# The Newton step of two layer norms moves from GpSimd to VectorE, in four fused operations

## The chip, the cores and the metric

The kernel runs on one core of one Trainium2 chip. The metric is the device time of one execution in microseconds (us); of several executions the median is taken. Engines are named as in the profile: PE is TensorE (matrix products), DVE is VectorE, ACT is ScalarE, POOL is GpSimd and SP is SyncE, which issues most of the transfers. PEld is TensorE's loading of weights, which runs beside its products.

## What is computed

The input x has 4 images of 64 x 64 tokens with 256 channels. Two layers follow each other. Cut to what matters:

```python
# layer 0: attention over the 4096 tokens of an image
f, g, v = xt @ Wf, xt @ Wg, xt @ Wh               # 32, 32 and 128 channels
beta = softmax(g @ f.T)                           # 4096 x 4096
x = x + (beta @ v) @ Wo

# layer 1: triangle attention, 8 heads of 32 channels, on the 64 x 64 grid of tokens
q, k, v1, v2 = x @ Wq, x @ Wk, x @ Wv1, x @ Wv2
att = softmax(einsum('bilhd,bljhd->biljh', q, k) / sqrt(32), axis=2)
out = einsum('biljh,bilhd,bljhd->bijhd', att, v1, v2)
h = layer_norm(x + out @ Wo)                      # the first norm
h = relu(h @ W1 + b1) @ W2 + b2 + h
return layer_norm(h)                              # the second norm
```

A layer norm needs for each token the mean m and the variance v over its 256 channels, and then r = 1/sqrt(v + eps). The kernel takes a first r from a logarithm and an exponential on ScalarE and improves it with one Newton step, r (1.5 - 0.5 (v + eps) r r). The normed value is r x + (-m r), one ScalarE operation with r and -m r as scale and bias.

## The kernel before

The kernel goes through the images. For each it does the attention, then the triangle, and into the triangle of an image it weaves other work: into that of image 0 the preparation of later images (order ORDER0), and into those of images 1 to 3 the rest of layer 1, the "pieces" of 256 tokens of the image before (order ORDER). The pieces of the last image come at the end, in a closing stage (`alone`).

The triangle of an image has 32 steps. A step makes eight products of a weight tile with v2, each 128 x 2048, and TensorE sums each with four selecting matmuls into PSUM. `npool` gives the last three products of an even step and the last two of an odd step to GpSimd, the others to VectorE. [...] ScalarE copies its share of the weights to SBUF (`copy_weights`).

```python
def product(self, step, m):
    ...
    if m >= 8 - k:                                          # k = npool(step)
        R = work.tile([P, D, N], F32, tag="Rp", name="Rp")  # two buffers
        eng, src = nc.gpsimd, attP[:, m - 8 + k, :]         # weights in SBUF
    else:
        R = work.tile([P, D, N], F32, tag="R", name="R", bufs=3)
        eng, src = nc.vector, att[:, n, ts(h, 64)]          # weights in PSUM
    v2 = self.v2[step // NIG]
    eng.tensor_tensor(R, src.unsqueeze(1).to_broadcast([P, D, N]), v2[:, h], ALU.mult)

def accumulate(self, step, m):
    ...
    for c in range(4):
        nc.tensor.matmul(acc[32 * c : 32 * c + 32, n % 2, :], w[:, n, c, 16 * h : 16 * h + 32], ...)

def copy_weights(self, step):
    ...
    nc.scalar.copy(attP[:, 0:k, :], att.rearrange(...)[:, 8 - k : 8, :])
```

The statistics, the root and the Newton step:

```python
def stats(self, src, k, ns=range(2)):                       # on VectorE
    for n in ns:
        nc.vector.bn_stats(st, src[:, n, :])
        nc.vector.bn_aggr(self.mv[:, k + n, :], st)

def sums_of(self, src, junk, mv, k):                        # on ScalarE: mean / 16, and the variance
    for n in range(2):
        nc.scalar.activation(junk[:, n, :], src[:, n, :], AF.Identity, scale=1.0 / (16 * C),
                             accum_out=mv[:, k + n, 0:1])
    for n in range(2):
        nc.scalar.activation(junk[:, n, :], src[:, n, :], AF.Square, bias=mv[:, k + n, 0:1],
                             scale=-1.0 / 16, accum_out=mv[:, k + n, 1:2])

def polish(self, k0, k1, eng, scale=1.0, back=None):        # the Newton step
    ...
    eng.tensor_scalar(t0, mv[:, :, 1], LN_EPS / scale, -0.5 * scale, ALU.add, ALU.mult)
    eng.tensor_tensor(t1, rs, rs, ALU.mult)
    eng.tensor_tensor(t1, t0, t1, ALU.mult)
    eng.tensor_scalar(t1, t1, 1.5, None, ALU.add)
    ...
    eng.tensor_tensor(r, t1, rs, ALU.mult)
    eng.tensor_tensor(nb, mv[:, :, 0], r, ALU.mult)
    if back is None:
        eng.tensor_scalar(nb, nb, -1.0, None, ALU.mult)
    else:
        eng.tensor_tensor(nb, nb, back[:, k0:k1], ALU.mult)
```

In the triangles of images 1 to 3 the first norm's statistics are taken by `stats`, the second's by `sums_of`, and `polish` runs on GpSimd for both norms at once (four columns). In the closing stage `polish` runs on VectorE with two columns, while GpSimd does `residue` and `finish`, two operations each on 128 x 512 elements.

The order in which the instructions of all engines are recorded is written by hand-made words. In ORDER, `R04/2` is the product m = 4 of the even step of a period, `R16` the product m = 6 of the odd step, `/2` says that it belongs to the work that began two periods earlier. A period is two steps and one piece. The other words: `A..` the summing of a product on TensorE, `T..` the taking of a sum from PSUM, `sp` a quarter of the scores and `e0 e1` their exponentials, `S.` the sums of the softmax, `W.` the weights, `t.` their transposes, `c.` copy_weights, `V.` the copy of v1; of the piece `h0 h1` the heads, `sa so` the statistics of the first and second norm, `rr` the roots, `pp` polish, `fa fo` the two affine operations, `ht` the transposes of the normed tile and `hU hT` what is read out of them, `m. r.` and `z.` the two layers of the perceptron, `fi` finish.

```python
ORDER = """
    r0/1 A10/2 A11/2 m1/1 R14/2 R05/1 S1/1 R15/2 T10/2 sp/1 A14/2 A16/2 r1/1 e0/1 e1/1 A15/2 A05/1 T11/2
    R04/1 A04/1 z0/1 W1/1 R03/1 V1/1 fi/2 S0 z1/1 t1/1 so/1 R06/1 R00/1 c1/1 sa A03/1 R07/1 R02/1 A06/1
    A02/1 A00/1 rr/1 pp/1 W0 R01/1 A07/1 A01/1 fo/1 fa T01/1 R12/1 t0 T00/1 R17/1 h1/-1 R13/1 h0/-1 ht
    R16/1 hU A13/1 hT A12/1 A17/1 R11/1 c0 R10/1 m0 V0
"""
```

Of the kernel before, what the change touches and what calls it, by code (L numbers as in the profile page):

```python
# [10 lines left out]
F32 = mybir.dt.float32  # L11
# [5 lines left out]
P = 128  # L17
# [21 lines left out]


ORDER = """
    r0/1 A10/2 A11/2 m1/1 R14/2 R05/1 S1/1 R15/2 T10/2 sp/1 A14/2 A16/2 r1/1 e0/1 e1/1 A15/2 A05/1 T11/2
    R04/1 A04/1 z0/1 W1/1 R03/1 V1/1 fi/2 S0 z1/1 t1/1 so/1 R06/1 R00/1 c1/1 sa A03/1 R07/1 R02/1 A06/1
    A02/1 A00/1 rr/1 pp/1 W0 R01/1 A07/1 A01/1 fo/1 fa T01/1 R12/1 t0 T00/1 R17/1 h1/-1 R13/1 h0/-1 ht
    R16/1 hU A13/1 hT A12/1 A17/1 R11/1 c0 R10/1 m0 V0
""".split()


# [13 lines left out]
def attention_then_triangle_kernel(  # L62
# [40 lines left out]
    nc.gpsimd.memset(ones_b, 1.0)  # L103
    ones_f = ctile([P, P], "ones_f")
    nc.gpsimd.memset(ones_f, 1.0)
    back_t = ctile([P, 4], "back")
    nc.gpsimd.memset(back_t, -1.0)
    nc.gpsimd.memset(back_t[:, 2:4], -16.0)
    eps_t = ctile([P, 1], "eps")
    nc.gpsimd.memset(eps_t, LN_EPS)  # L110

# [282 lines left out]
    def layer0(b, F, safe, rest):  # L394
# [250 lines left out]
        if old:  # L645
            rest.stats_a(t0)
            rest.roots(0, 2)
            rest.polish(0, 2, nc.gpsimd)
        bounds(last)
        proj(last, "v2", 0, None, stage[1][:, 0, :], nc.scalar)  # L650
        L.fetch_v2(0, 1)
# [234 lines left out]
    class Tokens:  # L886
# [69 lines left out]
                )  # L956


        def roots(self, k0, k1, scale=1.0):
            ln = small.tile([P, 4], F32, tag="ln", name="ln")  # L960
            nc.scalar.activation(ln[:, k0:k1], self.mv[:, k0:k1, 1], AF.Ln, bias=eps_t, scale=scale)
            self.rs = small.tile([P, 4], F32, tag="rs", name="rs")
            nc.scalar.activation(self.rs[:, k0:k1], ln[:, k0:k1], AF.Exp, scale=-0.5)


        def polish(self, k0, k1, eng, scale=1.0, back=None):
            mv, rs = self.mv[:, k0:k1], self.rs[:, k0:k1]
            t = small.tile([P, 2, 4], F32, tag="nt", name="nt")
            t0, t1 = t[:, 0, k0:k1], t[:, 1, k0:k1]
            eng.tensor_scalar(t0, mv[:, :, 1], LN_EPS / scale, -0.5 * scale, ALU.add, ALU.mult)  # L970
            eng.tensor_tensor(t1, rs, rs, ALU.mult)
            eng.tensor_tensor(t1, t0, t1, ALU.mult)
            eng.tensor_scalar(t1, t1, 1.5, None, ALU.add)
            self.rn = small.tile([P, 2, 4], F32, tag="rn", name="rn")
            r, nb = self.rn[:, 0, k0:k1], self.rn[:, 1, k0:k1]
            eng.tensor_tensor(r, t1, rs, ALU.mult)
            eng.tensor_tensor(nb, mv[:, :, 0], r, ALU.mult)
            if back is None:
                eng.tensor_scalar(nb, nb, -1.0, None, ALU.mult)
            else:  # L980
                eng.tensor_tensor(nb, nb, back[:, k0:k1], ALU.mult)
            self.mv = None

        def affine(self, dst, src, k, ns=range(2)):
# [97 lines left out]
        def alone(self, t0, t1):  # L1082
            V = nc.vector

            def normed(k0, k1):
                self.roots(k0, k1)
                self.polish(k0, k1, V)
# [36 lines left out]
            self.outputs(tt, 1, pc)  # L1124

            def summed(n):
                V.tensor_tensor(z[:, n], self.zp[tt + n][:, n], z[:, n], ALU.add)
                self.stats(z, 2, (n,))
                self.roots(2 + n, 3 + n)
                return self.mv, self.rs  # L1130

            def closed(n, known):
                self.mv, self.rs = known
                self.polish(2 + n, 3 + n, V)
# [16 lines left out]
    def step_words(L, fetched, stored):  # L1151
# [37 lines left out]
                L.copy_weights(step)  # L1189

        def scores(j):
            if j == 1:
                scores(0)
                L.take_scores()
            if 0 <= j < 12:
                L.scores(1 + j // 4, j % 4)
                sps[j] = L.sp
                if j % 4 == 3 and j // 4 + 2 < NPAIR:  # L1200
                    L.fetch_qk(j // 4 + 2)

        def take_scores(j, half):
            if 1 <= j < 12:
                L.sp = sps[j]
                L.take_scores(half)

# [8 lines left out]
    def first_layer1(L, ahead, F):  # L1216
# [30 lines left out]
        for period in range(NSTEP // 4 + 3):  # L1247
            for word, late in words_of(ORDER0):
                i, last = period - late, int(word[-1])
                if word[0:2] == "sp":  # L1250
                    if i >= 0:
                        scores(2 * i + 1 + last)
                elif word[0] == "e":
                    if i >= 0:
# [8 lines left out]
    def next_layer1(b, L, rest, ahead, F):  # L1263
# [32 lines left out]
        def of_piece(word, q):  # L1296
# [138 lines left out]
```

## Time and profile before

| | before |
|---|---|
| time, median of 3 runs | 3813.18 us (3807.73 to 3815.09) |
| span of the profiled execution | 3814.4 us |
| PE busy | 3687.0 us |
| DVE busy | 2639.6 us |
| ACT busy | 1930.3 us |
| POOL busy | 1804.2 us |
| accumulations of the triangles of images 0, 1, 2, 3, from and to | 502 to 925, 1379 to 1827, 2283 to 2733, 3187 to 3641 us |

A row of the groups reads: line, engine, operation, output and inputs with their sizes, count | busy time, mean of one in ns | idle time of the engine before them and what ended most of it. A row of a timeline reads: start, duration, engine, line, operation, count, and in brackets the idle time before it. L849 is the products, L859 the summing, L970 to L981 the Newton step, L1076 and L1077 `finish`, L1033 and L1034 `residue`.

### The profile page before, as it was taken

The numbers are of one execution on the slowest core, as the hardware profiler recorded it, in microseconds if no ns is written. First come the engines' busy times: TensorE is split into PE (matmuls) and PEld (weight loads), VectorE is DVE, ScalarE is ACT, GpSimd is POOL, SyncE is SP. The second block draws the span as 40 slices with busy tenths as digits, with TensorE's granted clock in tenths as the row PEclk, the third lists the DMA queues.
The fourth block names the chain that finished last, engine by engine and source line by source line (L and its number), as shares of the span: only waits on it lengthen the run. The fifth ranks groups of instructions, "written<-read, shape, count | busy, mean of one in ns | idle before, by whom it ended". The sixth has DMA issues, their size and how long they took to land.

```text
span 3814.4 us, 60208 instructions
## 1 busy us (share of the span) xinstructions
PE 3687.0 (97%) x23498; PEld 1800.0 (47%) x23498; DVE 2639.6 (69%) x2050; ACT 1930.3 (51%) x4257; POOL 1804.2 (47%) x930
## 2 busy tenths in 40 slices
PE   9999989898999999999999999999999999999997
PEld 5444444443444455554344444555344445555476
DVE  4444479997544459999544448999754455999976
ACT  3333355554333356776333346766533335677654
POOL 4000079996000049999100008999600004999944
PEclk9999999999999999999999999999999999999999
DMA  4111355544111164313111153342211116431221
GB/s 117 54 50 50 95 145 147 142 124 139 38 46 53 53 152 94 89 49 93 61 50 47 53 126 83 83 95 70 92 42 47 50 59 144 95 88 48 69 61 51
DMA packets 439750, 309.44 MB, mean 81 GB/s; under 512 B 299360, under 2 KB 404576, under 8 KB 432160
## 3 DMA queue, kind: packets, MB, share of 16 engines
q1 hardware_dynamic: 419952, 291.12, 29.1%
q10 hardware_dynamic: 16240, 8.59, 0.8%
q0 software_dynamic: 3264, 5.78, 0.7%
q8 instruction: 188, 3.08, 0.4%
q14 instruction: 106, 0.87, 0.1%
HBM read 165.88 MB, written 139.46 MB: 80 GB/s over the span
## 4 chain that ended last, share of the span: by engine, by line
PE 79%; POOL 5%; DVE 5%; DMA 4%; issue 4%; ACT 2%; SPq 1%; ACTq 0%; DVEq 0%; POOLq 0%
PE o L469 24%; PE acc L859 16%; PE proj L526 8%; PE s L447 7%; PE mp L1042 5%; PE zp L1062 4%; POOL Rp L849 4%; DVE R L849 3%; PE v1p L551 3%; PE sp L747 3%; PE hp L918 2%; DMA xin<-in_x_dram 2%; PE y L511 2%; PE att L801 1%; PE den L486 1%
## 5 line engine op out<-in xcount | busy, mean ns | idle before, releaser
L849 POOL TENSOR_TENSOR Rp<-attP,v 128x2048 f32<-128x2048 f32 x328 | 1490.1, 4575 | 459.0 <-ACT attP L809 385.2
L849 DVE TENSOR_TENSOR R<-att,v 128x2048 f32<-128x2048 f32 x696 | 1546.4, 2274 | 111.3 <-PE acc L859 77.8
L476 DVE TENSOR_TENSOR esum<-esum,e 128x2048 f32<-128x2048 f32 x224 | 512.8, 2289 | 586.2 <-ACT e L458 582.6
L859 PE MATMUL acc<-R,wsel 128*32 128x512 f32 x5568 | 706.4, 605 | 37.2 <-DVE R L849 25.5
L458 ACT ACTIVATE e<-s 128x1024 f32<-128x1024 f32 x512 | 496.5, 1021 | 406.5 <-PE s L447 391.9
L970 POOL TENSOR_SCALAR nt<-mv 128x4 f32<-128x4 f32 (+1 forms) x51 | 9.9, 193 | 1286.2 <-DVE mv L935 1282.4
L469 PE MATMUL o<-e,vlo 128*128 128x512 f32 x1024 | 477.0, 609 | 0.0
L469 PE MATMUL o<-e,vhi 128*128 128x512 f32 x1024 | 472.6, 605 | 0.0
L859 PE MATMUL acc<-Rp,wsel 128*32 128x512 f32 x2624 | 349.8, 605 | 12.9 <-POOL Rp L849 12.3
L869 ACT COPY ao<-acc 128x1024 f32<-128x1024 f32 x256 | 254.1, 1020 | 198.0 <-PE acc L859 135.9
L859 PEld LDWEIGHTS acc<-R,wsel 128*32 128x32 f32 x5568 | 153.7, 110 | 370.6 <-issue 269.8
L469 PEld LDWEIGHTS o<-e,vlo 128*128 128x128 f32 x1024 | 185.1, 191 | 283.0 <-issue 283.0
L469 PEld LDWEIGHTS o<-e,vhi 128*128 128x128 f32 x1024 | 184.3, 189 | 279.7 <-issue 279.7
L447 PE MATMUL s<-gT,fT 32*128 32x512 f32 x2048 | 302.2, 640 | 4.3 <-ACT e L458 3.9
L784 ACT ACTIVATE es<-S,rd 128x64 f32<-128x64 f32 x1024 | 257.7, 336 | 3.4 <-ACT stage L538 2.6
L488 DVE RECIPROCAL rec<-den 128x512 f32<-128x512 f32 x32 | 107.4, 3358 | 215.6 <-PE den L486 215.6
L1062 PE MATMUL zp<-w,hid 128*128 128x256 f32 x1024 | 247.6, 387 | 7.5 <-ACT hid L1051 7.5
L1042 PE MATMUL mp<-hT,w 128*128 128x256 f32 x1024 | 249.5, 389 | 0.7 <-ACT hT L1014 0.7
L1042 PEld LDWEIGHTS mp<-hT,w 128*128 128x128 f32 x1024 | 186.5, 190 | 101.9 <-ACT attP L809 36.0
L1062 PEld LDWEIGHTS zp<-w,hid 128*128 128x128 f32 x1024 | 186.5, 191 | 72.2 <-issue 31.9
L538 ACT COPY st<-proj 128x512 f32<-128x512 f32 x104 | 60.9, 585 | 293.2 <-issue 165.9
L859 PEld LDWEIGHTS acc<-Rp,wsel 128*32 128x32 f32 x2624 | 81.3, 111 | 202.0 <-issue 138.2
(166 smaller groups left out, 3832.7 us busy)
## 6 DMA issues: line engine op xcount, KB each, us to landing
v<-v2d SPq DMA_DIRECT2D x24, 1024.0 KB, 12.7
v1c<-v1d SPq DMA_DIRECT2D x128, 128.0 KB, 2.9
aT<-ao SPq DMA_DIRECT2D x1024, 16.0 KB, 1.9
A<-aT SPq DMA_DIRECT2D x256, 64.0 KB, 2.1
out_dram<-z SPq DMA_DIRECT2D x63, 256.0 KB, 2.5
y<-yT SPq DMA_DIRECT2D x56, 256.0 KB, 2.1
q<-st SPq DMA_DIRECT2D x56, 256.0 KB, 2.6
v1d<-st SPq DMA_DIRECT2D x56, 256.0 KB, 2.2
```

The source lines that it names most:

```text
L447: nc.tensor.matmul(s_ps[r // 2][:, r % 2, :], fT[rows, tt, ts(n, P)], gT[rows, ts(qb, QB)], start=True, stop=not safe,)
L458: nc.scalar.activation(e[g][:, 2 * j : 2 * j + 2, :], s_ps[j], AF.Exp)
L469: nc.tensor.matmul(o_ps[qb], F.v[tt][:, r * 4 + n, :], es[:, r, :], start=(k == 0 and r == 0), stop=(k == 7 and r == 3),)
L476: nc.vector.tensor_tensor(esum[qb], esum[qb], es, ALU.add)
L526: nc.tensor.matmul(ps, w[:, cc, rows], y(qb, cc), start=(cc == 0), stop=(cc == 1))
L551: nc.tensor.matmul(ps[:, ts(n, C)], y(qb, cc)[:, ts(m * 2 + n, P)], wv1_sb[:, cc, :], start=(cc == 0), stop=(cc == 1),)
L784: nc.scalar.mul(e[:, i, :], rows[:, i, :], rec[:, i : i + 1])
L849: eng.tensor_tensor(R, src.unsqueeze(1).to_broadcast([P, D, N]), v2[:, h], ALU.mult)
L859: nc.tensor.matmul(acc[32 * c : 32 * c + 32, n % 2, :], w[:, n, c, 16 * h : 16 * h + 32], R[:, ts(c, 8), :].rearrange("p d j -> p (d j)"), ...
L869: nc.scalar.copy(self.ao[step][:, ts(np, 2)].rearrange("p k d j -> p k (d j)"), self.acc[step][np])
L1042: nc.tensor.matmul(self.mp[:, fc % 2, :], w1_sb[:, cc, ts(fc, P)], self.hT[tt][:, cc, :], start=(cc == 0), stop=(cc == 1),)
L1062: nc.tensor.matmul(zp[:, n, :], self.hid[tt][:, fc, ts(n, P)], w2_sb[:, fc, :], start=(fc == 0), stop=(fc == 3 and tt not in self.hT2),)
```

## The change

The Newton step is written as four operations of the form (a op scalar) op b, always on VectorE. The factor that brings the mean back from mean / 16 becomes part of the last of them. For this both norms must have their statistics in the same form, so in the triangles of images 1 to 3 the first norm's are now taken by ScalarE too. This takes the step off GpSimd and the batch-norm statistics off VectorE, and makes the step shorter in operations. The quarters of the scores are numbered from zero, so that each period has one and the first is no exception. The words of ORDER stand in a new order for these new loads. ORDER0, the attention and the image-0 triangle keep theirs.

```diff
 ORDER = """
-    r0/1 A10/2 A11/2 m1/1 R14/2 R05/1 S1/1 R15/2 T10/2 sp/1 A14/2 A16/2 r1/1 e0/1 e1/1 A15/2 A05/1 T11/2
-    ...
+    A12/3 V0/2 sp/2 T10/3 m1/2 e0/2 R17/3 R02/2 e1/2 A02/2 r1/2 R15/3 A16/3 R14/3 A15/3 R00/2 c0/2 A17/3
+    sa/1 A14/3 S0/1 fi/3 R03/2 T11/3 z1/2 S1/1 z0/2 t1/2 R05/2 A03/2 W0/1 R01/2 so/2 rr/2 R04/2 c1/2
+    R06/2 A05/2 pp/2 A01/2 V1/2 A06/2 A00/2 A04/2 R13/2 R10/2 R07/2 fo/2 t0/1 fa/1 R16/2 h1 ht/1 T00/2
+    hU/1 R11/2 h0 A07/2 hT/1 A13/2 R12/2 A10/2 W1/1 T01/2 m0/1 A11/2 r0/1
 """.split()
...
-        def polish(self, k0, k1, eng, scale=1.0, back=None):
-            mv, rs = self.mv[:, k0:k1], self.rs[:, k0:k1]
+        def polish(self, k0, k1, part=1.0):
+            mv, rs, V = self.mv[:, k0:k1], self.rs[:, k0:k1], nc.vector
             ...
-            eng.tensor_scalar(t0, mv[:, :, 1], LN_EPS / scale, -0.5 * scale, ALU.add, ALU.mult)
-            eng.tensor_tensor(t1, rs, rs, ALU.mult)
-            eng.tensor_tensor(t1, t0, t1, ALU.mult)
-            eng.tensor_scalar(t1, t1, 1.5, None, ALU.add)
             ...
-            eng.tensor_tensor(r, t1, rs, ALU.mult)
-            eng.tensor_tensor(nb, mv[:, :, 0], r, ALU.mult)
-            if back is None:
-                eng.tensor_scalar(nb, nb, -1.0, None, ALU.mult)
-            else:
-                eng.tensor_tensor(nb, nb, back[:, k0:k1], ALU.mult)
+            V.scalar_tensor_tensor(t0, mv[:, :, 1], LN_EPS, rs, ALU.add, ALU.mult)
+            V.scalar_tensor_tensor(t1, t0, -0.5, rs, ALU.mult, ALU.mult)
+            V.scalar_tensor_tensor(r, t1, 1.5, rs, ALU.add, ALU.mult)
+            V.scalar_tensor_tensor(nb, mv[:, :, 0], -1.0 / part, r, ALU.mult, ALU.mult)
...
             elif word == "sa" and first:
                 moments(q - 1)
-                rest.stats(rest.hps[t0 + q], 0)
+                h = rest.h[tt] = work.tile([P, 2, C], F32, tag="h", name="h", bufs=1)
+                rest.sums_of(rest.hps[tt], h, rest.mv, 0)
...
             elif word == "pp" and second:
                 moments(q)
                 rest.rs = rs.pop(q)
-                rest.polish(0 if q + 1 < n1 else 2, 4, nc.gpsimd, back=back_t)
+                rest.polish(0 if q + 1 < n1 else 2, 4, 1.0 / 16)
...
                 elif word == "sp":
-                    if i >= 1:
-                        scores(i)
+                    scores(i)
```

More of the change, by code (lines that the diff above doesn't have):

```diff
@@ L41 @@
 ORDER = """
-    r0/1 A10/2 A11/2 m1/1 R14/2 R05/1 S1/1 R15/2 T10/2 sp/1 A14/2 A16/2 r1/1 e0/1 e1/1 A15/2 A05/1 T11/2
-    R04/1 A04/1 z0/1 W1/1 R03/1 V1/1 fi/2 S0 z1/1 t1/1 so/1 R06/1 R00/1 c1/1 sa A03/1 R07/1 R02/1 A06/1
-    A02/1 A00/1 rr/1 pp/1 W0 R01/1 A07/1 A01/1 fo/1 fa T01/1 R12/1 t0 T00/1 R17/1 h1/-1 R13/1 h0/-1 ht
-    R16/1 hU A13/1 hT A12/1 A17/1 R11/1 c0 R10/1 m0 V0
+    A12/3 V0/2 sp/2 T10/3 m1/2 e0/2 R17/3 R02/2 e1/2 A02/2 r1/2 R15/3 A16/3 R14/3 A15/3 R00/2 c0/2 A17/3
+    sa/1 A14/3 S0/1 fi/3 R03/2 T11/3 z1/2 S1/1 z0/2 t1/2 R05/2 A03/2 W0/1 R01/2 so/2 rr/2 R04/2 c1/2
+    R06/2 A05/2 pp/2 A01/2 V1/2 A06/2 A00/2 A04/2 R13/2 R10/2 R07/2 fo/2 t0/1 fa/1 R16/2 h1 ht/1 T00/2
+    hU/1 R11/2 h0 A07/2 hT/1 A13/2 R12/2 A10/2 W1/1 T01/2 m0/1 A11/2 r0/1
 """.split()
@@ L105, in attention_then_triangle_kernel @@
     nc.gpsimd.memset(ones_f, 1.0)
-    back_t = ctile([P, 4], "back")
-    nc.gpsimd.memset(back_t, -1.0)
-    nc.gpsimd.memset(back_t[:, 2:4], -16.0)
     eps_t = ctile([P, 1], "eps")
@@ L647, in layer0 @@
             rest.roots(0, 2)
-            rest.polish(0, 2, nc.gpsimd)
+            rest.polish(0, 2)
         bounds(last)
@@ L956, in sums_of, with roots @@
                 )
[L959 removed]
+        def roots(self, k0, k1):
             ln = small.tile([P, 4], F32, tag="ln", name="ln")
[L961 removed]
+            nc.scalar.activation(ln[:, k0:k1], self.mv[:, k0:k1, 1], AF.Ln, bias=eps_t)
             self.rs = small.tile([P, 4], F32, tag="rs", name="rs")
             nc.scalar.activation(self.rs[:, k0:k1], ln[:, k0:k1], AF.Exp, scale=-0.5)
[L966 to L967 removed]
+        def polish(self, k0, k1, part=1.0):
+            mv, rs, V = self.mv[:, k0:k1], self.rs[:, k0:k1], nc.vector
             t = small.tile([P, 2, 4], F32, tag="nt", name="nt")
             t0, t1 = t[:, 0, k0:k1], t[:, 1, k0:k1]
[L970 to L973, printed above, removed]
             self.rn = small.tile([P, 2, 4], F32, tag="rn", name="rn")
             r, nb = self.rn[:, 0, k0:k1], self.rn[:, 1, k0:k1]
[L976 to L981 removed]
+            V.scalar_tensor_tensor(t0, mv[:, :, 1], LN_EPS, rs, ALU.add, ALU.mult)
+            V.scalar_tensor_tensor(t1, t0, -0.5, rs, ALU.mult, ALU.mult)
+            V.scalar_tensor_tensor(r, t1, 1.5, rs, ALU.add, ALU.mult)
+            V.scalar_tensor_tensor(nb, mv[:, :, 0], -1.0 / part, r, ALU.mult, ALU.mult)
             self.mv = None
@@ L1086, in normed @@
                 self.roots(k0, k1)
-                self.polish(k0, k1, V)
+                self.polish(k0, k1)
             def turn(tt):
@@ L1133, in closed @@
                 self.mv, self.rs = known
-                self.polish(2 + n, 3 + n, V)
+                self.polish(2 + n, 3 + n)
                 self.affine(z, z, 2, (n,))
@@ L1193, in scores @@
         def scores(j):
-            if j == 1:
-                scores(0)
-                L.take_scores()
             if 0 <= j < 12:
@@ L1203, in take_scores @@
         def take_scores(j, half):
-            if 1 <= j < 12:
+            if 0 <= j < 12:
                 L.sp = sps[j]
@@ L1251, in first_layer1 @@
                     if i >= 0:
+                        if i == last == 0:
+                            scores(0)
+                            for half in range(2):
+                                take_scores(0, half)
                         scores(2 * i + 1 + last)
```

## Prediction

> **What bounds the kernel now.** I read the busy table first, then the busy time by stretch, the groups, and the timeline of single engines.
>
> ```profile
> PE 3687.0 (97%) x23498; PEld 1800.0 (47%) x23498; DVE 2639.6 (69%) x2050; ACT 1930.3 (51%) x4257; POOL 1804.2 (47%) x930
> ...
> L849 POOL TENSOR_TENSOR Rp<-attP,v 128x2048 f32<-128x2048 f32 x328 | 1490.1, 4575 | 459.0 <-ACT attP L809 385.2
> L849 DVE TENSOR_TENSOR R<-att,v 128x2048 f32<-128x2048 f32 x696 | 1546.4, 2274 | 111.3 <-PE acc L859 77.8
> ...
> L970 POOL TENSOR_SCALAR nt<-mv 128x4 f32<-128x4 f32 (+1 forms) x51 | 9.9, 193 | 1286.2 <-DVE mv L935 1282.4
> ```
>
> TensorE is busy for 97% of the span, so only its idle 3814.4 - 3687.0 = 127 us can be won. But the averages hide a stage in which three engines are full. The change touches the triangles of images 1 to 3 and the closing stage; a row of the next table is a 50 us stretch with PE, PEld, DVE, ACT and POOL busy.
>
> ```profile
> 1550.00:1600.00 50.00, 50.00 (x472) 27.66 (x468) 48.20 (x36) 35.94 (x98) 47.71 (x28) 1.00 0.41 92
> ...
> 3650.00:3700.00 50.00, 48.90 (x244) 42.46 (x244) 39.49 (x115) 26.37 (x70) 23.40 (x19) 1.00 0.27 73
> ```
>
> In a triangle, VectorE (48.20) and GpSimd (47.71) are within 5% of TensorE (50.00). A period (two steps, one piece of the tokens) takes 27.76 us, the distance between successive Newton steps in GpSimd's timeline; the last four take 27.2. GpSimd's side of one period:
>
> ```profile
> 1511.64 0.20 POOL L981 TENSOR_TENSOR rn<-rn,back 128x4 f32<-128x4 f32 x1
> 1511.79 13.66 POOL L849 TENSOR_TENSOR Rp<-attP,v 128x2048 f32<-128x2048 f32 x3
> 1525.37 1.31 POOL L1076 TENSOR_TENSOR z<-z,log_bc 128x512 f32<-128x512 f32 x1
> 1526.76 1.29 POOL L1077 TENSOR_TENSOR z<-z,lob_bc 128x512 f32<-128x512 f32 x1
> 1528.50 9.10 POOL L849 TENSOR_TENSOR Rp<-attP,v 128x2048 f32<-128x2048 f32 x2 [0.46 <-PE acc L859]
> ```
>
> To be seen: products follow each other without a gap, one per 13.66/3 = 4.55 us. Now what VectorE's small operations cost while GpSimd works, from the closing stage (start, duration, engine):
>
> ```profile
> 3666.71 0.16 DVE L971 TENSOR_TENSOR nt<-rs 128x2 f32<-128x2 f32 x1
> 3666.78 1.27 POOL L1077 TENSOR_TENSOR z<-z,lob_bc 128x512 f32<-128x512 f32 x1
> 3666.91 1.15 DVE L972 TENSOR_TENSOR nt<-nt 128x2 f32<-128x2 f32 x1
> ...
> 3668.01 1.27 POOL L1033 TENSOR_TENSOR z<-h,lag_bc 128x512 f32<-128x512 f32 x1
> ...
> 3668.10 1.20 DVE L973 TENSOR_SCALAR nt<-nt 128x2 f32<-128x2 f32 x1
> 3669.33 0.16 DVE L976 TENSOR_TENSOR rn<-nt,rs 128x2 f32<-128x2 f32 x1
> 3669.35 1.28 POOL L1034 TENSOR_TENSOR z<-z,lb_bc 128x512 f32<-128x512 f32 x1
> 3669.53 1.12 DVE L977 TENSOR_TENSOR rn<-mv,rn 128x2 f32<-128x2 f32 x1
> ```
>
> L972 has two columns and needs 0.16 us when left alone, yet takes 1.15: it ends at 3668.06, when GpSimd's L1077 does (3668.05). L973 and L977 likewise end with L1033 and L1034. GpSimd is not delayed. An operation slips in between (L971, L976) only where GpSimd has a gap, as between L1076 and L1077, the second of which needs the first. Between L1077 and L1033, which start back to back, one VectorE operation gets through and the next waits for the whole of L1033.
>
> **What the Trainium skill says.** "SBUF — State Buffer", section "Who interferes with whom": a VectorE instruction with two SBUF inputs contends with a GpSimd instruction that reads SBUF, and whichever starts second is blocked until the first ends. The trace agrees (1.15 us for a 0.16 us operation). It also explains why VectorE's products (2274 ns) don't suffer: one of their inputs lies in PSUM. "Perfetto Trace Analysis", section "GPSIMD Engine Instruction", advises start-to-start spacing over reported spans; hence 4.55 us here. "VectorE: DVE Perf Modes", section "Rules for kernel authors", says to minimize the number of operations; the change does, but in the triangle it is the wait that counts. "PSUM — Partial Sum Buffer", section "PSUM bank collisions raise a hardware error", forbids ScalarE and VectorE in one bank at once, and the built program keeps to it: a ScalarE copy of weights waits for the VectorE products recorded before it.
>
> **The change part by part.**
> GpSimd loses seven Newton operations a period: 1509.94 to 1511.79 in its timeline, 1.85 us. With them gone its period is 5 x 4.55 + 2.65 = 25.4 us.
> VectorE loses two pairs of statistics, 1532.79 to 1533.95, 1.16 us. It gains four small operations, 0.2 us each in the closing stage (L972 to L973: 3663.15 to 3663.35), 0.8 us if nothing blocks them. ScalarE gains about 1.9 us (the same four statistics of the second norm: 1507.39 to 1509.27) on 19.9 of 27.8; it has room.
> TensorE's work per period is the same, and so is the number of its changes between 32-column and 128-column work (four runs of accumulation in both orders). No gain there. The quarters of the scores move by one word, with all else one period later; I give it nothing.
> So on paper everything but the Newton step gets lighter. But all its four operations read two SBUF tensors (mv and rs, nt and rs, mv and rn), and in the new order they stand behind the product R04 on VectorE while GpSimd does R06, R07 and R16.
>
> The new period, as an estimate from the durations above, with 0 at the end of a Newton step:
> - VectorE does R13, R10, R11, R12, R02, R15, R14, R00: 8 x 2.21 = 17.7 (13.28/6 = 2.21 in its timeline). ScalarE's c0 copies R05's weights out of the same PSUM bank, and in the built program waits for R00: 18.1.
> - R05 starts at 18.2. R05, R06, R07, R16 end at 22.8, 27.3, 31.9 and 36.4, if TensorE frees their buffers in time. It does: from 0 come the norm's affine operations on ScalarE 2.0, ht 0.5, h0 1.1, A07 A13 A10 2.7 (an A is 0.86), m0 1.9, A11 A12 1.9, sp 1.9, m1 1.9, A02 A16 1.9, so A16, which frees R05's buffer, by about 16; A17 by 18, A05 by 25, A06 by 28.
> - VectorE meanwhile: sums 0.8, R03 20.8, sums 0.8, R01 23.8, R04 (needs A03, about 24.1) 26.4. The root is there by 25.4: TensorE's z words end at 22.5, and W0, the statistics and two activations keep ScalarE until then. The first operation arrives in the middle of R06.
> - First operation done at 27.3 with R06, second at 31.9 with R07, third at 36.4 with R16. The next product, R17, needs the buffer of A07, which stands on TensorE behind the transpose of the normed tile, so behind this very step: GpSimd is idle and the fourth passes. End: 36.7 us.
> TensorE then waits some 9 us a period. Its own 27.8 us lie beside this.
> The first and last Newton steps of a triangle stand at 1391.6 and 1813.2 (2297.5 and 2720.9; 3199.7 and 3624.0): 15 distances, 421.6 + 423.4 + 424.3 = 1269.3 us. After: 3 x 15 x 36.7 = 1651.5. Difference +382. Start and end of a triangle: about +5 each for the first blocked step and the later last products, +15.
> Closing stage: seven operations from 3665.51 to 3670.85 become four, of which perhaps three are blocked: 1 to 2 us less per piece. But the piece (10.33 us) holds about 9.9 us of TensorE work, so at most 0.4 x 15 = 6, I take -5.
> Sum: 3813 + 382 + 15 - 5 = 4205.
>
> **Rivals.**
> A: two operations slip through at one boundary. Then the step ends with R07 at about 32.1, 15 x 32.1 = 481.5 per image, +212, near 4020. For it: L971 and L976. Against: these slip where GpSimd has a gap, and products have none.
> B: no blocking of the fused form. Then the chain A02, R00, c0, R05, R06, A06, around TensorE back to A02, is 2.3 + 0.5 + 9.1 + 17.1 = 29.0 us (17.1 being TensorE's 27.8 less the 10.7 from A16 to A01) in the 12 periods with scores, 27.2 without: at most +45, 3810 to 3860. For it: the only fused operation of this kind before (L512, 743 ns) reads PSUM, so the trace has no case. Against: L972 and L977 are blocked for their two SBUF inputs, and the fused ones have them too.
> C: the change works as meant: 1.85 us off GpSimd frees the last four periods and the fill, 3 x 4 x about 1.3 = 16 us, 3795. For it: the last four periods are exactly GpSimd's sum (27.2). Against: as B, and c0.
>
> **Range and chances.** I give about 0.7 to the full blocking (4150 to 4250), 0.2 to A or a mixture, 0.1 to B and C. I put the prediction at 4190, a little under the sum for A's sake; 3990 to 4240 should hold it 8 times in 10. Faster by over 2% 0.01, within 2% 0.07, slower by over 2% 0.92.
>
> **What will show it.** In the changed profile the four fused operations should have means of microseconds instead of 0.2, several near 4.5, and end together with GpSimd's products; the step should come every 36 to 37 us in triangles 1 to 3; TensorE's busy share should fall to about 88%, with waits of ScalarE's norms for rn and of TensorE for h at the transposes. The image-0 triangle and the attention stages should stay as they are. Fused operations of 0.2 us in the triangle would prove me wrong (B); steps every 32 us would be A; and if GpSimd's products rather than VectorE's operations were delayed, the mechanism would be turned around.

## The result and the profile after

The changed kernel takes 4304.56 us (median of 4 runs, 4302.66 to 4310.92) against 3814.14 us (3807.73 to 3815.23) for the kernel before: a ratio of 1.129, 95% interval 1.127 to 1.131. It is slower, as predicted; the size is 114 us above the predicted 4190 and outside the range.

The page of the kernel after, busy times and groups (L846 are the products, L969 to L972 the fused step, L977 the affine operations, L915 the heads' products on TensorE); behind them two rows of the groups with different shapes kept apart:

```profile
PE 3802.0 (88%) x23498; PEld 1862.0 (43%) x23498; DVE 3055.9 (71%) x1974; ACT 2001.9 (47%) x4625; POOL 1728.5 (40%) x571
...
L846 POOL TENSOR_TENSOR Rp<-attP,v 128x2048 f32<-128x2048 f32 x328 | 1483.9, 4556 | 2364.0 <-ACT attP L806 1637.9
L846 DVE TENSOR_TENSOR R<-att,v 128x2048 f32<-128x2048 f32 x696 | 1553.2, 2278 | 176.5 <-PE acc L856 143.2
...
L977 ACT ACTIVATE z<-zp,rn 128x256 f32<-128x256 f32 x98 | 50.0, 560 | 499.9 <-DVE rn L972 499.9
```

```profile
L970 DVE SCALAR_TENSOR_TENSOR nt<-nt,rs 128x4 f32<-128x4 f32 x46 | 203.9, 4433 | 1.6
L971 DVE SCALAR_TENSOR_TENSOR rn<-nt,rs 128x4 f32<-128x4 f32 x46 | 189.4, 4117 | 1.6
```

The second and the third operation have means of 4433 and 4117 ns on four columns, the first and the fourth 1060 and 162 ns. ScalarE's affine operation waits 499.9 us for the step's last result. GpSimd, from the first to the last accumulation of images 1 to 3, is busy for 1178.3 of 1826.7 us, where it was busy for 1262.5 of 1343.5; the 2364 us of idle time in the table include the attention stages. The products themselves cost what they did (4556 and 2278 ns). TensorE's busy time has grown by 115 us for the same 23498 matmuls; the experiments come back to that.

Busy time by stretch (PE, PEld, DVE, ACT, POOL), the same place in a triangle and one in the closing stage:

```profile
1550.00:1600.00 50.00, 34.99 (x283) 19.46 (x272) 47.57 (x24) 24.00 (x67) 32.56 (x9) 0.86 0.12 30
...
4150.00:4200.00 50.00, 50.00 (x252) 43.89 (x251) 34.39 (x93) 27.71 (x74) 25.20 (x20) 1.00 0.30 82
```

VectorE still shows 47.57 of 50 us busy, but much of it is waiting inside its own operations; TensorE has fallen to 34.99 and GpSimd to 32.56. In the timeline of VectorE one sees a whole period's step:

```profile
1660.70 2.29 DVE L846 TENSOR_TENSOR R<-att,v 128x2048 f32<-128x2048 f32 x1 [0.33 <-PE acc L856]
1662.91 0.72 DVE L969 SCALAR_TENSOR_TENSOR nt<-mv,rs 128x4 f32<-128x4 f32 x1
1663.66 4.46 DVE L970 SCALAR_TENSOR_TENSOR nt<-nt,rs 128x4 f32<-128x4 f32 x1
1668.16 4.42 DVE L971 SCALAR_TENSOR_TENSOR rn<-nt,rs 128x4 f32<-128x4 f32 x1
1672.61 0.16 DVE L972 SCALAR_TENSOR_TENSOR rn<-mv,rn 128x4 f32<-128x4 f32 x1
1672.69 6.69 DVE L846 TENSOR_TENSOR R<-att,v 128x2048 f32<-128x2048 f32 x3
1680.77 2.29 DVE L846 TENSOR_TENSOR R<-att,v 128x2048 f32<-128x2048 f32 x1 [1.39 <-PE acc L856]
```

and in that of GpSimd what stands beside it, four products R05, R06, R07, R16 back to back:

```profile
1654.52 18.03 POOL L846 TENSOR_TENSOR Rp<-attP,v 128x2048 f32<-128x2048 f32 x4 [5.83 <-ACT attP L806]
1680.02 4.56 POOL L846 TENSOR_TENSOR Rp<-attP,v 128x2048 f32<-128x2048 f32 x1 [7.46 <-PE acc L856]
```

The four products end near 1659.1, 1663.6, 1668.1 and 1672.55. L969, L970 and L971 end at 1663.63, 1668.12 and 1672.58, so one VectorE operation gets through at each boundary. This holds throughout: all 135 operations on four columns that took over 0.3 us end within 0.03 us of the end of a GpSimd operation. L972 has GpSimd idle and takes 0.16 us. The step takes 9.9 us in place of the 1.85 it took on GpSimd, and everything behind it waits.

From span to span (3814.4 to 4301.8, +487.4 us; a triangle's stretches are taken from TensorE's accumulations and the starts of the steps; the first accumulations of images 1 to 3 before the change are at 1382.4, 2286.6 and 3190.4 us, some 3 us later than the table of the profile before has them):

| stretch | predicted | measured |
|---|---|---|
| 15 distances between steps, images 1 to 3 | +382 | 568.1 + 569.1 + 570.1 - 1269.2 = +438.1 |
| last accumulation of an image to the first of the next, 3 times | together | (464.4 - 457.1) + (465.0 - 458.9) + (463.8 - 456.7) = +20.5 |
| first accumulation to first step, and last step to last accumulation | +15 | +0.8, and 15.6 + 17.2 + 11.7 = +44.5 |
| closing stage, last accumulation to the end | -5 | 173.1 to 159.9 = -13.2 |
| up to the end of image 0's triangle | 0 | 925.2 to 921.9 = -3.3 |

### The profile page after: what moved, and what is told of

Read it like the earlier page. It is cut to its first block, busy times and chain, and to the rows that moved or that the text cites. A ratio compares the mean times of both kernels' runs of the same rounds, so it can differ in the third digit from the quotient of the medians.

```text
span 4301.8 us, 60334 instructions
## 1 busy us (share of the span) xinstructions
PE 3802.0 (88%) x23498; PEld 1862.0 (43%) x23498; DVE 3055.9 (71%) x1974; ACT 2001.9 (47%) x4625; POOL 1728.5 (40%) x571
## 5 line engine op out<-in xcount | busy, mean ns | idle before, releaser
L846 POOL TENSOR_TENSOR Rp<-attP,v 128x2048 f32<-128x2048 f32 x328 | 1483.9, 4556 | 2364.0 <-ACT attP L806 1637.9
L846 DVE TENSOR_TENSOR R<-att,v 128x2048 f32<-128x2048 f32 x696 | 1553.2, 2278 | 176.5 <-PE acc L856 143.2
L856 PE MATMUL acc<-R,wsel 128*32 128x512 f32 x5568 | 715.8, 612 | 35.9 <-DVE R L846 31.3
L915 PE MATMUL hp<-wo,A 128*128 128x256 f32 x512 | 195.8, 521 | 289.5 <-ACT z L977 289.5
L977 ACT ACTIVATE z<-zp,rn 128x256 f32<-128x256 f32 x98 | 50.0, 560 | 499.9 <-DVE rn L972 499.9
L915 PEld LDWEIGHTS hp<-wo,A 128*128 128x128 f32 x512 | 125.4, 268 | 320.8 <-ACT z L977 300.9
L970 DVE SCALAR_TENSOR_TENSOR nt<-nt,rs 128x4 f32<-128x4 f32 (+2 forms) x83 | 231.5, 2790 | 2.8
```

What stands on the lines that cost most here:

```text
L915: nc.tensor.matmul(hp[:, n, :], A[:, cc, ts(n, 2), :].rearrange("p i j -> p (i j)"), wo1_sb[:, cc, :], start=(cc == 0), stop=False,)
L970: V.scalar_tensor_tensor(t1, t0, -0.5, rs, ALU.mult, ALU.mult)
```

## Experiments

The theory on trial: an operation of VectorE that reads two SBUF tensors is held by GpSimd's products (the expectations call this the shared port), and this alone makes the kernel slow. Its rivals: the new order, the dependency of c0 on R00, and the statistics on ScalarE. Where no interval is given, the time is that of one execution; the kernel before took 3808.99 to 3812.77 us beside these. A period is the usual distance between steps: 37.9 us in the kernel after (median of 45), where some expectations still have 38.3.

**The step back on GpSimd, all else as changed.**

```diff
-                rest.polish(0 if q + 1 < n1 else 2, 4, 1.0 / 16)
+                rest.polish_pool(0 if q + 1 < n1 else 2, 4, 1.0 / 16)   # seven operations on GpSimd
```

> The changed kernel, with the Newton step of the triangles of images 1 to 3 back on GpSimd in seven operations (same new ORDER, same statistics on ScalarE). Theory 1, the shared port: the four fused operations are blocked by GpSimd's products, so without them a period falls from 38.3 us to about 29.3 (eight VectorE products, c0, R05, R06 and the step of 1.85 us), and the time to about 3870 us (3840 to 3920). Theory 2, the new order of words is to blame by itself: it stays above 4200 us. Theory 3, the extra statistics on ScalarE are to blame: also above 4200 us.

Measured: 3902.6 us, a step every 30.05 us. 402 of the 490 us are gone with the place of the step alone. What remains is a second cause: in each period ScalarE's copy of weights waits about 2.4 us for a VectorE product, and GpSimd's product 2.6 us for that copy.

**The old order, with the step on VectorE and both statistics on ScalarE.**

```diff
-    A12/3 V0/2 sp/2 ...            (ORDER of the changed kernel, and its numbering of the quarters)
+    r0/1 A10/2 A11/2 ...           (those of the kernel before)
```

> The kernel before with its own ORDER, but with the fused Newton step on VectorE and both norms' statistics by ScalarE, as in the change. Theory 1 (shared port): the step now stands among GpSimd's R07, R17 and R16 and two or three of its operations wait 4.5 us each; 4100 to 4350 us. Theory 2 (the new order is to blame): about 3800 to 3830 us, with fused operations of 0.2 us.

Measured: 4315.2 us, a step every 38.7 us. On four columns its first two operations have means of 2688 and 4232 ns, the last two of 162. The order isn't the culprit: the old one is as slow with this step.

**The same arithmetic on VectorE with one SBUF tensor per operation.** The other factor goes in as a scalar per partition, so one fused operation becomes four of one column: 16 in place of 4.

```diff
-            V.scalar_tensor_tensor(t0, mv[:, :, 1], LN_EPS, rs, ALU.add, ALU.mult)
-            ...
+            for k, s in cols:
+                V.tensor_scalar(t[:, 0, s], mv[:, k, 1:2], LN_EPS, rs[:, s], ALU.add, ALU.mult)
+            ...
```

> The changed kernel, with the Newton step of the triangles as 16 operations on single columns on VectorE, in the same place; each reads one SBUF tensor, the other factor is a per-partition scalar operand. Theory 1 (two SBUF tensors take the port that GpSimd holds): each takes about 0.16 us, the step about 3 us, a period 29.5 to 30 us, the time about 3880 us (3850 to 3930), although there are four times as many operations. If any small VectorE operation waits for GpSimd, or if a scalar operand takes the same port, there are 16 waits instead of three and the time is well above 4300 us. If the order is to blame: about 4300 us.

Measured: 3880.13 us, period 29.28. GpSimd's timeline, four products without a break, and VectorE's beside it:

```profile
1657.98 18.17 POOL L846 TENSOR_TENSOR Rp<-attP,v 128x2048 f32<-128x2048 f32 x4
```

```profile
1661.87 0.57 DVE L981 TENSOR_SCALAR nt<-mv,rs 128x1 f32<-128x1 f32 x4
1662.35 0.57 DVE L983 TENSOR_SCALAR nt<-nt,rs 128x1 f32<-128x1 f32 x4
1662.84 0.57 DVE L985 TENSOR_SCALAR rn<-nt,rs 128x1 f32<-128x1 f32 x4
1663.32 0.57 DVE L987 TENSOR_SCALAR rn<-mv,rn 128x1 f32<-128x1 f32 x4
1663.81 13.37 DVE L846 TENSOR_TENSOR R<-att,v 128x2048 f32<-128x2048 f32 x6
```

Sixteen operations take 1.94 us where four took 9.9; none of the 752 of this form is held (mean 203 ns, at most 212). Same engine, same place in the order, same arithmetic: the 424 us belong to the form of the operations. But the run changes three things in that form, the number of SBUF tensors (two to one), of columns (four to one) and the kind of instruction. The trace of the kernel before tells them apart in part. It has reciprocals with one SBUF tensor on eight columns:

```profile
L776 DVE RECIPROCAL rd<-dens 128x8 f32<-128x8 f32 x128 | 26.0, 203 | 6.5 <-ACT es L784 1.6
```

All take 202 to 205 ns, the 116 among them that start while GpSimd works too, so it isn't the columns; and plain TENSOR_TENSOR operations with two SBUF tensors are held (L972 in the prediction; all 13 that start beside GpSimd take 1.15 to 1.19 us), so it isn't the fused form. One SBUF tensor is not always free, though: L973 in the prediction's timeline, a TENSOR_SCALAR with constants on two columns, reads one and was held 1.19 to 1.20 us all 12 times that it started beside GpSimd. So two SBUF tensors are enough to be held: in the kernels before and after, every small operation with two that started during a product, `finish` or `residue` of GpSimd was. Why L973 is held and the one-column operations of this run are not, no run shows.

**Shorter GpSimd products.** If the wait is for the end of a product, halves and quarters of it must shorten the wait in step.

```diff
-            eng.tensor_tensor(R, src.unsqueeze(1).to_broadcast([P, D, N]), v2[:, h], ALU.mult)
+            parts = 2 if eng is nc.gpsimd and self.b > 0 else 1          # 4 in the second run
+            ...                                                          # one tensor_tensor for each part
```

> The changed kernel, in which GpSimd makes each product in the triangles of images 1 to 3 in two operations of 128x1024 (about 2.4 us each, worked out from 1.28 us for 512 and 4.55 for 2048 columns). Theory 1 (a fused operation waits for the end of the GpSimd operation under way): the waits fall to about 2.4 us but the fourth operation now waits too; from arrival at 28.7 us the four pass at 29.7, 32.1, 34.5 and 36.9, period about 37.0 us, time about 4240 us (4220 to 4265). Rival (GpSimd's products themselves are what is late, and the waits of the fused operations only show it): GpSimd gets slower by 0.2 us per product, so the time rises, 4320 to 4350.

> The same with four operations of 128x512 (1.28 us each). Theory 1: waits of 1.28 us at most, the four pass at about 29.3, 30.5, 31.8 and 33.1, period about 33.2 us, time about 4060 us (4030 to 4095), although GpSimd works 0.58 us longer on each product. Rival: 0.58 x 4 products on the path of each period, above 4380 us.

| GpSimd product | four-column fused operations, mean us | period, us | time, us |
|---|---|---|---|
| whole, 4.55 us | 1.06, 4.43, 4.12, 0.16 | 37.9 | 4304.56 |
| halves | 1.19, 2.27, 2.25, 2.26 | 36.7 | 4222.36 |
| quarters | 0.49, 1.16, 1.18, 1.19 | 30.55 | 3936.57 |

The operations follow the length of the part. With halves the fourth operation is held too, and the step ends with the first half of R16, so little is won; with quarters it ends 12 us before the row of products does. The second run gained 124 us more than I expected, because I had scaled the wait and not seen that the step then ends well ahead of R16.

**The second cause.** c0 copies R05's weights out of the bank that R00 reads, and is recorded behind R00. Moved ahead of it, with the step on GpSimd:

```diff
-    ... R14/3 A15/3 R00/2 c0/2 A17/3
+    ... R14/3 A15/3 R00/2 A17/3
     ...
-    hU/1 R11/2 h0 A07/2 hT/1 A13/2 R12/2 A10/2 W1/1 T01/2 m0/1 A11/2 r0/1
+    hU/1 R11/2 h0 A07/2 hT/1 A13/2 R12/2 A10/2 W1/1 T01/2 c0/1 m0/1 A11/2 r0/1
```

> The new ORDER with the Newton step on GpSimd (as in e1: 3902.6 us) and with c0, ScalarE's copy of R05's weights, moved to right behind T01, so that it no longer waits for the product R00. Theory: without blocking, the new order is held at 29 to 30 us a period by the chain A02, R00, c0, R05, R06, A06; with c0 early that chain is 27.2 and TensorE's 27.8 bounds the period again; 3795 to 3825 us. If the chain through c0 is not what holds it: 3880 to 3910 us.

Measured: 3821.21 us, ratio 1.0024 (1.0014 to 1.0035), period 28.26. This chain costs some 80 us once the blocking is gone (3902.6 to 3821.2); it is the prediction's rival B, hidden behind the blocking in the changed kernel. The version with sixteen operations, nearest to rival B, has a period of 29.28 us, where B had 29.0, and 3880.13 us, above B's 3810 to 3860. No run has that step and the early c0 together, so that its remaining 66 us are this chain is argued. The rest of the new order is then within 0.4% of the old.

**Why the period is 37.9 and not 36.7.** The timeline of TensorE, kernel after (L798 weights, L915 the heads h1, L1000 the transposes), and in single microseconds the granted clock, as a share of TensorE's full clock (third number from the end):

```profile
1666.38 0.66 PE L798 MATMUL att<-ident,es 128*128 128x128 f32 x4
1673.88 2.07 PE L915 MATMUL hp<-wo,A 128*128 128x256 f32 x4 [6.85 <-ACT z L977]
...
1676.17 1.06 PE L1000 MATMUL htp<-ident,h 128*128 128x128 f32 x4
```

```profile
1670.00:1671.00 1.00, 0.00 (x0) 0.00 (x0) 1.00 (x1) 0.00 (x0) 1.00 (x1) 1.00 0.00 0
1672.00:1673.00 1.00, 0.00 (x0) 0.00 (x0) 0.97 (x3) 0.19 (x1) 0.56 (x1) 0.50 0.00 0
1677.00:1678.00 1.00, 1.00 (x5) 0.82 (x4) 1.00 (x2) 0.68 (x2) 0.00 (x0) 0.50 0.00 0
1679.00:1680.00 1.00, 1.00 (x12) 0.26 (x8) 0.38 (x1) 1.00 (x5) 0.00 (x0) 1.00 0.19 44
```

Two suspects: h1 needs a buffer that the affine operation behind the step releases, and the clock that TensorE gets behind this wait is half. First the heads, moved behind A02, and in a second run behind A17:

```diff
-    ... R02/2 e1/2 A02/2 r1/2 R15/3 ...        and  ... R16/2 h1 ht/1 ... R11/2 h0 A07/2
+    ... R02/2 e1/2 A02/2 h1/1 h0/1 r1/2 R15/3  and  ... R16/2 ht/1 ... R11/2 A07/2
```

> The changed kernel, with the heads h1 and h0 moved in ORDER from around the transposes to behind A02. It tests the part of the period that the prediction had too small (38.3 us against 36.7). Theory 1a: h1 waits for the affine operation of the second norm (its PSUM buffer), and it and the transposes run at half speed after TensorE's wait of 7 us, so A02, and with it R00 and c0, come 1.6 us late; with the heads out of that path the period is 36.7 to 37.3 us and the time about 4230 us (4215 to 4265). Theory 1b, the 1.6 us come from something else (the waits between the products, GpSimd's own length): 4290 to 4315 us.

> The changed kernel with h1 and h0 behind A17 instead of behind A02, so that A16 (which frees R05's buffer) is no longer behind them; in the run before, R00 came 15.6 us after the step's end, as the prediction had it, but R05 then waited for A16 until 19.1. Theory 1a: R00 15.6, R05 about 18.4, period 36.8 to 37.1 us, time about 4240 us (4220 to 4260). If the size of the period hangs on something else: 4270 to 4305.

Measured: 4271.1 and 4269.68 us, both between the two ranges; period 37.5 in both. In the first, R00 was back at 15.6 us behind the step's end, but R05 then waited for A16, which now stood behind the heads, until 19.1; in the second R05 started at 18.5, as meant, but R07 waited 0.59 us for A05. Both keep the wait and the half clock, only at the transposes (a wait of 7.2 us in the first). So these runs don't decide.

Next TensorE was given work during the wait: matmuls with zero weights that add zero to a sum that is still open.

```diff
+                if word == "h1" and 0 <= period - 2 < NP:      # "ht" in the runs with the heads moved
+                    L.keep_busy(2 * (period - 2), 11)          # 11 x 4 matmuls of zero weights; later 6 x 4
```

> The changed kernel, with 44 matmuls of zero weights (11 groups of 4, about 5.7 us, adding zero to a sum that is open) put on TensorE ahead of the heads, where it waited 6.85 us for the affine operation. If the half clock behind that wait is what makes the period longer than predicted: the granted clock stays at 1.00, the four products of h1 take 1.03 us instead of 2.07, about 2 us of lateness go, most of the waits of R12 and R00 with them, the period falls from 37.9 to about 36.9, and the time to 4255 (4230 to 4275). If the place of the heads alone does it (rival), clock and products change as said but the time stays at 4290 to 4310.

> The same 44 matmuls in the version with the heads behind A02 (4271.1 us, period 37.5, clock at half behind each wait for the transposes), put ahead of the transposes. With both causes gone the predicted timeline should hold: period 36.7, so 45 x 0.8 = 36 us less, 4235 (4215 to 4250). If the clock does not matter (rival): 4262 to 4278.

Measured: 4340.5 and 4271.7 us. I had mis-sized the added work: a matmul of this kernel shows as two records, so 44 of them took 9.65 us instead of 5.7 and outlasted the wait. The clock stayed at 1.00, but TensorE came late, so the runs give no verdict, though 4271.7 lies in the rival's range. Again with 24:

> The changed kernel with 24 zero-weight matmuls (48 records, 48 x 0.11 = 5.3 us) ahead of the heads; they end about 2 us before the affine operation does. If the half clock makes the difference: clock 1.00 all through, h1's four products at 1.13 us instead of 2.07, the wait of R12 falls from 1.39 to under 0.5 us, period 36.7 to 37.1, time 4304.6 - 45 x 1.0 = about 4260 (4235 to 4275). If only the place of the heads does (rival): 4290 to 4310.

> The same 24 matmuls ahead of the transposes in the version with the heads behind A02 (4271.1 us, period 37.5). If the half clock makes what is left of the difference, the period is the 36.7 of the prediction and the time 4235 (4215 to 4250). If not (rival): 37.5 and 4262 to 4278; then what holds R05 in that version is the heads' own 2.8 us on TensorE ahead of A16.

Measured: 4217.77 and 4273.79 us. The first, in the timelines of TensorE and of VectorE:

```profile
1656.73 5.36 PE L870 MATMUL acc<-wo,none 128*32 128x512 f32 x48
1663.72 1.13 PE L927 MATMUL hp<-wo,A 128*128 128x256 f32 x4 [1.64 <-ACT z L989]
1664.69 0.38 PE L932 MATMUL hp<-ident,yc 128*128 128x128 f32 x2
1664.91 0.60 PE L1012 MATMUL htp<-ident,h 128*128 128x128 f32 x4
```

```profile
1662.53 17.74 DVE L848 TENSOR_TENSOR R<-att,v 128x2048 f32<-128x2048 f32 x8
```

The clock reads 1.00 in every stretch from 1660 to 1692, h1 takes 1.13 us instead of 2.07, and VectorE's eight products run without a gap in 17.74 us (the prediction's timeline had 17.7). The period is 36.46 us. With the same order, h1 still behind the affine operation, and 24 matmuls more per period, the kernel is 87 us faster, 77 of them in the 45 distances between steps (1707.3 to 1629.9 us): it was the half clock that put the period above 36.7. The kernel after agrees without any addition. In periods 2 to 11 of an image, those with 6.83 us at half clock take 37.8 to 38.5 us and those with 10.24 us take 39.3; with the clock kept they take 36.4 to 36.5.

The second run's 4273.79 us lie in the rival's range. The clock fell all the same (0.64 in 1676 to 1680, behind a wait of 2.02 us), though for half as long as without the added work (3.41 us in most periods instead of 6.83), and the period stayed at 37.5. With the heads moved, R05 starts 19.0 to 19.3 us behind the step's end at either clock. So nothing there speaks for the clock; what it costs in that version stays open.

**The score quarters from zero.** In the changed kernels TensorE waits ahead of the first accumulation of a triangle for the transfer of q and k. Tried both ways: the old numbering in the version with the step on GpSimd and c0 early, and the new numbering alone in the kernel before.

```diff
-                    if i >= 1:
-                        scores(i)
+                    scores(i)                 # and no scores(0) inside scores(1); the reverse in the other run
```

> The changed kernel with its step on GpSimd and c0 early (3821.2 us) and the old numbering of the score quarters. In the changed kernels TensorE waits about 5.9 us before the first accumulation of each of three triangles, because quarter 0 now stands ahead of it and waits for the transfer qk<-k. If the numbering causes this, the gap between the last accumulation of an image and the first of the next goes back from 463.9, 463.4, 463.2 to about 457, the first period takes 4 us (a quarter and a wait for ScalarE) back, and the time falls by about 3 x 3 = 9 us: 3808 to 3814, ratio to the kernel before 0.9985 to 1.0005. If the new order causes it (rival), the gap stays near 463 and the time at 3818 to 3824.

> The kernel before with the score quarters numbered from zero and nothing else changed. If quarter 0 in the first period has to wait for the transfer qk<-k, the gap before the first accumulation of the triangles grows from 457 to 461 to 465 us, a wait of TensorE at the scores for qk appears (none before), the first period loses about 4 us, and the time rises by 3 to 12 us: ratio 1.001 to 1.003. If the wait belongs to the new order (rival), the gap stays and the time falls by up to 3 x 2 = 6 us, ratio 0.9985 to 1.0000.

Measured: 3814.2 us, ratio 1.0011 (1.0003 to 1.0019), and 3804.87 us, ratio 0.9989 (0.9982 to 0.9995). The wait belongs to the numbering. In the kernel before with the new numbering alone:

```profile
PE sp L747 <- DMA qk<-k: 17.6, 6, 4.5
```

(total us, times, longest), and the gap before the first accumulation grows to 464 us. But the first period takes it back: the 15 distances come to 414.9 us instead of 421.5 in the first of these triangles. I had expected 4 us back per triangle and it was 6.6 to 9.4, so the sign of my estimate for the second run was wrong. In the other version the profile shows the exchange alike (a gap near 457, but distances of 428 instead of 421). A matter of a few us either way.

**The parts that could be gains.** The fused step in the closing stage only, everything else as before:

```diff
-                self.polish(k0, k1, V)
+                self.polish4(k0, k1)          # the four fused operations; likewise in closed()
```

> The kernel before, with the fused Newton step in the closing stage alone (the triangles keep their ORDER, VectorE's statistics and GpSimd's seven operations). In the changed kernel the closing stage, from the last accumulation to the end, took 160.6 us against 173.7 before. Theory: the gain there is the step's own, as four operations meet fewer of GpSimd's four; 3801 us, ratio 0.9966 (0.995 to 0.998). Rival, as the prediction had it: TensorE's work bounds the piece and at most 6 us can be won; ratio 0.9985 or more.

Measured: 3801.58 us, ratio 0.9968 (0.9956 to 0.998). The stage falls from 173.1 to 160.1 us. Added to that, the first norm's statistics on ScalarE, in the old order and with the step on GpSimd:

```diff
-                rest.stats(rest.hps[t0 + q], 0)
+                rest.sums_of(rest.hps[tt], h, rest.mv, 0)
```

> The same, and in the triangles of images 1 to 3 the first norm's statistics by ScalarE as in the change, with the old ORDER and the Newton step on GpSimd in seven operations. Theory: VectorE loses 1.16 us a period and ScalarE gains 1.9, both beside TensorE's 27.8, so nothing changes against the run before: ratio 0.9950 to 0.9985. Rival (the extra statistics delay the roots and with them the step): periods longer than 27.8 us, ratio above 1.005.

Measured: 3839.37 us, ratio 1.0059 (1.0045 to 1.0073); the rival holds. GpSimd's timeline of that kernel:

```profile
1504.16 9.11 POOL L849 TENSOR_TENSOR Rp<-attP,v 128x2048 f32<-128x2048 f32 x2
1514.58 0.20 POOL L984 TENSOR_SCALAR nt<-mv 128x4 f32<-128x4 f32 x1 [1.32 <-ACT h L953]
1515.15 0.20 POOL L985 TENSOR_TENSOR nt<-rs 128x4 f32<-128x4 f32 x1 [0.37 <-ACT rs L963]
```

GpSimd now waits 1.32 us for ScalarE's statistics and 0.37 for the root. Its period was 27.2 us of work, so these 1.7 us make it 28.9, and 28.93 is measured: the statistics left VectorE, which had room, and came onto the path of GpSimd, which had none.

Last, the two gains together, the fused step in the closing stage and the quarters from zero:

> The kernel before with the fused step in the closing stage only (alone 0.9968) and the score quarters from zero (alone 0.9989). The two lie in different stages, so they should add up: ratio 0.9957 (0.9945 to 0.9968), about 3797 us. If the start of the triangles gives back what the closing stage wins, or the reverse (rival), the ratio stays at 0.997 or above.

Measured: 3795.22 us, ratio 0.996 (0.9946 to 0.9973), against 3810.66 us of the kernel before beside it. They add up, and this version is 0.4% faster than the kernel before.

## Why the prediction was right in kind and too small

**The blocking.** Right, in its detail: the first operation ends with R06, the second with R07, the third with R16, and the fourth passes. That the form with two SBUF tensors is the reason is shown by the sixteen one-input operations together with the reciprocals of the kernel before, and that a product's end is what is waited for by halves and quarters. The Trainium skill's "SBUF — State Buffer", section "Who interferes with whom", also says that a VectorE instruction with at most one SBUF input, outside the 2-port performance modes, doesn't contend with GpSimd. The sixteen operations and the reciprocals agree (0.20 us). L973 has one input and was held 1.20 us, which the prediction, naming it beside L977, passed over; whether it ran in such a mode, no run here shows. Rival A (two operations slip at a boundary) happened in none of the 46 steps on four columns; rival C is ruled out.

**The period.** The step that failed is "if TensorE frees their buffers in time. It does: from 0 come ...". Each term of that line was taken at full clock. But the prediction itself had TensorE wait "some 9 us a period", and behind that wait the clock is at half until 1678, so A13 and A02 came late, R12 waited 1.39 us, R00 started at 17.5 instead of 15.5 us and R05 at 20.2 instead of 18.2. The line also left out h1, which stands behind the affine operation. With the clock kept and h1's place unchanged, R05 starts at 18.15 and the period is 36.46 against the 36.7 of the prediction.

In sums: the 45 distances came to 438 us more than before, 56 above the 382 of the prediction. With the clock kept they come to 1629.9 - 1269.2 = 361 more, 21 below it. So the half clock (77 us in these distances) more than explains what was missing there. That the 4217.77 us of that run lie so near the sum of 4205 is partly luck: starts and ends of the triangles, treated next, were 40 us above the estimate in it and make up for the 21 and the closing stage.

The cost was there to be read: "TensorE: Matmul & The Clock Gate", section "What's actually happening", says that an idle window of about 3.4 us halves the clock and that sustained work of as long releases it. The trace agrees: work ended at 1667.03, the clock was still 1.00 in 1670 to 1671 and 0.50 in 1672; h1 began at 1673.88 and the clock was 1.00 again by 1679.

**Start and end of a triangle.** Mis-sized: "about +5 each" was +22 per triangle. The last step finds GpSimd products in a row: five in images 1 and 2, where all four of its operations are held (15.9 us), and four in image 3 (11.1 us), against 1.9 before. I had not followed this through; it is most of the +44.5. The other +20.5 is the wait for q and k. In the kernel before with the new numbering alone the first period gives it back; if it does here too, it is only a shift, and that I gave the numbering "nothing" was about right.

**Closing stage.** Right in direction, -13.2 instead of -5. The term that failed is "the piece (10.33 us) holds about 9.9 us of TensorE work": it holds 9.51. Where TensorE doesn't wait, pieces follow each other every 9.51 us in the kernel before already (its first products of the heads start at 3661.93 and 3671.44). After the change, nine pieces that took 10.2 to 10.4 us take 9.51, and the 50 us stretch above shows TensorE busy for 50.00.

**Range and weights.** Lowering the sum of 4205 to 4190 for rival A's sake moved it the wrong way, and A's own sum was off (3 x 481.5 - 1269.3 is 175, not 212, so about 4000); the range's upper end of 4240 left 35 us above the sum, for a timeline in which nothing that comes late had a term of its own.

## What to carry to other kernels

Count an operation's SBUF tensors before its instructions: beside a GpSimd that never stops, sixteen operations with a per-partition scalar cost 1.94 us where four with two tensors cost 9.9. Check a one-tensor operation in the trace all the same, as L973 was held. When a change makes TensorE wait for several microseconds, price the work behind the wait at half clock; here that was 18% of the loss, and 24 matmuls of zero weights in the gap won it back. The number must fit the gap: 44 of them made the kernel 36 us slower, and with the heads moved 24 won nothing. Test the parts of a bundled change alone: two of its parts were gains of 0.3% and 0.1%, hidden under a loss of 13%.

## What the runs showed of the hardware that I had not expected

- The half clock as a cost at the scale of the kernel: the same 23498 matmuls count 3802.0 us busy instead of 3687.0, and adding 24 matmuls per period made the kernel 87 us faster.
- The granted clock changes on a grid. In all traces here, every stretch between two changes is a whole multiple of 3.413 us: at half clock mostly 6.83 or 10.24 us in the kernel after, mostly 3.41 us in the run with 24 zero-weight matmuls ahead of the transposes.
- In that run the clock fell behind a wait of only 2.02 us, while behind one of 1.64 us, in the run with the heads in place, it didn't. Of the idle window of about 3.4 us in the page cited above, 2.02 us are only a part. Where a wait falls on the grid may decide this; what is counted isn't settled by these runs.
- A fused operation on 128x4 elements was held for 4.4 to 4.5 us, as long as a whole product, again and again: between GpSimd's back-to-back products just one VectorE operation gets through each time.
